# A four-layer graph stack on one core: the order of the small work among the first tiles, and neighbour counts on four quarters of the PE array

## The chip, the cores and the metric

The kernel runs on one core of one Trainium2 chip. The metric is device time in microseconds of the whole launch. A core has five engines with queues of their own: PE (matmul, with its weight loads shown apart as PEld), DVE (VectorE), ACT (ScalarE), POOL (GpSimd) and SP (SyncE, which here only issues DMAs).

## The reference

The graph has N = 3327 nodes with D = 64 features, `x` [N, D], and a dense matrix `adj` [N, N] of which well under 1% of the entries are not zero (all f32). Four layers follow each other, each `x = x + layer(relu(layernorm(x)))`:

```python
# layer 0: two gated cells, relu after each
m = adj @ (x @ W);  gi = m @ wih.T + bih;  gh = x @ whh.T + bhh
r = sigmoid(i_r + h_r); z = sigmoid(i_z + h_z); n = tanh(i_n + r * h_n)
x = (1 - z) * n + z * x
# layer 1: weights by the rank of a neighbour in its row
mask = (adj != 0);  rank = cumsum(mask, axis=1);  deg = rank[:, -1:]
k = minimum(deg, 100);  pos = rank - (deg - k)
w = mask * where(pos > 0, 0.5 ** (k - pos), 0);  out = w @ (x @ weight) + bias
# layer 2: three times  x = ((adj * adj) @ x) @ W.T + b
# layer 3: twice        x = tanh(concat([adj @ x, x]) @ W[k])
```

So `adj` is multiplied from the left eight times, k = 0 to 7 in the kernel. Layer 1 (k = 2) needs, for each row and each block of 128 columns, how many neighbours lie in later blocks: the counts that the change touches.

## The kernel before

The host pads `adj` to 3328 and passes it transposed. A node index is (s, b, p): half s of 2, block b of 13, position p of 128. Output nodes are cut into four chunks of blocks, `CH` = 0-3, 3-6, 6-9, 9-13, and into two groups of chunks, `GROUPS = [(0, 1), (2, 3)]`. A tile of `adj` is 128 sources q (26 of them) by the outputs of one group in both halves: 128 x 2 x 768 f32 for group 0 (768 KB), 128 x 2 x 896 for group 1 (896 KB). It lands in one of 20 slots. `propagate` (L607) multiplies a tile, chunk by chunk, into PSUM sums: the features of the 128 sources are the weights (128 x 64), the tile streams, and half s of the outputs goes to half s of the PE columns. Each f32 product is two passes in the trace, so a tile costs eight passes, four per chunk.

The loop: a list `units` of (k, chunk, tile) is written before anything is issued. `alone(0, 0, ...)` puts product k = 0 for group 0, `joint(1, 0, ...)` puts k = 0 for group 1 with k = 1 for group 1 a few tiles behind (`later`), so that a tile serves two products, and so on. The last `sweep` tiles go chunk by chunk. `run()` walks through `units`, issues loads up to 44 units ahead, masks (`make_mask`, L466: VectorE turns a tile into 0/1 bf16, in two halves), and then calls `propagate`. Small work stands in generators (`tasks`), advanced by `spend`, which charges PE time to each task: a `yield 1.5` waits for 1.5 us of products to be issued. Thus every engine's order of instructions is fixed when the program is written out; on the chip only semaphores decide when each starts. Loads are all on SP's queue in that order, with at most eight DMAs in flight (each waits for the one eight before it).

The counts: during k = 0, `count` (L542) multiplies each masked tile by `behind`, a 128-row matrix of ones and zeros whose window of D columns starts at NQ - 1 - q (NQ = 26). Row i of the result for half s sums over all tiles with q > i. For each of the two chunks of a group and each half there is one product with 64 weight columns (of which at most 26 carry counts) into PSUM rows `s * D`, and one bank per chunk. `Counting` holds `lag` tiles back and then issues one tile's counts after each tile. At the end `count_done` (L555) copies a bank to `totals`.

Before the first product: `before_0(c)` calls `layernorm_relu` (L834 to L849; the reciprocal root is on POOL, L845) for chunk c, then `transpose_to_features` (L791, ACT copies L793). The start-up loop `for c in (0, 0, 1, 0, 1, 2, 1, 2, 3, 2, 3, 3)` advances the four of them in turn. `more_constants` clears buffers on POOL, loads the cell weights (`load_cell`, L152 and L155, into `stage`), unfolds them (L162, copies L165, L167), folds two matrices (L175, L307), and computes one gate of the first cell ahead of time for each chunk (`ahead_of_cell`, L201). When k = 0 of a chunk ends, `after_0` runs its cell: `evacuate_stacked` (L824, L825), gates (L876), elementwise work (L881 to L908), back to nodes (L774, L944).

Of the kernel before, what the change touches and what calls it, by code (L numbers as in the profile page):

```python
# [44 lines left out]
N, D = 3327, 64  # L45
P = 128
NB = 13
NQ = 2 * NB
# [3 lines left out]
CH = [(0, 3), (3, 6), (6, 9), (9, 13), (3, 5), (5, 6)]  # L52
NC = 4
PARTS = (4, 5)
CWM = 512
GROUPS = [(0, 1), (2, 3)]
# [24 lines left out]
STREAM_US = 0.86  # L81
# [15 lines left out]
def kernel(  # L97
# [9 lines left out]
    nc = tc.nc  # L107
# [18 lines left out]
    stage = const.tile([P, 7 * D + NBIAS], F32, name="stage")  # L126
# [24 lines left out]
    def load_cell(cell):  # L151
        nc.sync.dma_start(out=stage[upper(0), :7 * D].rearrange("p (w f) -> p w f", f=D),  # L152
                          in_=weights[:, (W1, W2)[cell]:(W1, W2)[cell] + 7])
        if cell == 0:
            nc.sync.dma_start(out=stage[upper(0), 7 * D:], in_=bias_cols)  # L155
# [80 lines left out]
        yield from product(1, 2)  # L236

    def more_constants():
        nc.gpsimd.memset(stage, 0.0)
        nc.gpsimd.memset(cells, 0.0)  # L240
        for c in range(NC):
            for h in range(2):
                nc.gpsimd.memset(both[c][upper(h), h], 0.0)
        nc.gpsimd.memset(bd, 0.0)
        yield 5.0
        load_cell(0)
        yield 20.0
        unfold_cell(0)
        yield 1.0

        full = work.tile([P, P], BF16, name="t2")
        nc.gpsimd.memset(full, -TWO7)
        nc.gpsimd.affine_select(out=tri, in_=full, pattern=[[-1, P]], compare_op=ALU.is_gt, fill=0.0,
                                base=0, channel_multiplier=1)
        nc.gpsimd.affine_select(out=tri, in_=tri, pattern=[[-1, P]], compare_op=ALU.not_equal, fill=TWO7 * TWO7,
                                base=0, channel_multiplier=1)
        nc.gpsimd.memset(tri[:, P - 1:P], 0.0)
        nc.gpsimd.memset(bitsb, BITS)
        nc.gpsimd.memset(lasty, 0.0)
        wide = work.tile([P, P], F32, name="t2")  # L260
        nc.gpsimd.memset(wide, 0.0)

        for i, (bi, bh) in enumerate(((BI1, BH1), (BI2, BH2))):
            nc.vector.tensor_add(bsum[:, i], bcol[:, bi:bi + 2], bcol[:, bh:bh + 2])

        nc.vector.tensor_scalar(wide[0:D], wide[0:D], bcol[0:D, BL1:BL1 + 1], None, op0=ALU.add)
        yield 3.0
        i, ps = take()
        mm(ps[:, :D], wide, ident[:, :D])
        nc.vector.tensor_copy(brow[:, 3], ps[:, :D])  # L270
        give(i)
        yield 1.0
        yield from fold_cell(0)
        for c in range(NC):
            yield 1.0
            ahead_of_cell(c)
        yield 50.0
        load_cell(1)
        yield 20.0
        unfold_cell(1)  # L280
        yield from fold_cell(1)
        yield 30.0
        for h in range(2):
            nc.sync.dma_start(out=bd[upper(h), :, upper(h)], in_=weights[:, WL1:WL3])
            for i in range(2):
                nc.sync.dma_start(out=w3[upper(h), :, i], in_=weights[:, WL3 + (h + i) % 2:NW:2])
        yield 5.0
        nc.sync.dma_start(
            out=brow[:, 0:3],
            in_=bass.AP(tensor=bias_rows.tensor, offset=bias_rows.offset, ap=[[0, P], [D, 3], [1, D]]),  # L290
        )
        yield 22.0
        yield from fold_hops()
# [5 lines left out]
    def width(c):  # L299
        return blocks(c) * P  # L300
# [15 lines left out]
    def take(sums=False, either=True):  # L316


        either = either and not sums
        pool = idle_sums if sums else idle_temps  # L320
        if either and idle_sums and (not pool or released[idle_sums[0]] < released[pool[0]]):
            pool = idle_sums
        for c in list(tasks):
            if not pool and c not in running:
                advance(c)
        i = pool.popleft()
        return i, banks[i]
# [33 lines left out]
    def begin(c, task):  # L361
        finish(c)
        tasks[c] = [task, 0.0]
        advance(c)

    def finish(c):
        while c in tasks:
            advance(c)

    def later_task(us, task):  # L370
        yield us
        yield from task

    def spend(us):

        for c in list(tasks):
            if c in tasks and c not in running:
                tasks[c][1] -= us
                if tasks[c][1] <= 0:
                    advance(c)  # L380
# [79 lines left out]
    def make_mask(t, kind):  # L460

        t.mask = Mask(t.w)
        rows = P - 1 if kind == RANKED else P

        def piece(half):
            nc.vector.tensor_scalar(t.mask.view[:rows, half], t.view()[:rows, half], 0.0, None, op0=ALU.not_equal)  # L466
            if half == 0 and kind == RANKED:

                for ch in GROUPS[t.g]:
                    finish(("count", ch))  # L470
                nc.gpsimd.dma_start(out=t.mask.view[P - 1:P], in_=totals[t.g][t.q:t.q + D + 1:D, :])  # L471
            if half == 1:
                t.used()

        pieces.extend([(t, 0, piece), (t, 1, piece)])
# [54 lines left out]
    counts = {}  # L530
    squared = {}

    def count(t, first, last):


        mask_pieces(t=t)
        for c in GROUPS[t.g]:
            w = width(c)
            if first:
                counts[c] = take(either=False)  # L540
            for s in range(2):
                nc.tensor.matmul(counts[c][1][s * D:(s + 1) * D, :w], behind[:, NQ - 1 - t.q:NQ - 1 - t.q + D],  # L542
                                 t.mask.view[:, s, t.cols(c)], start=first, stop=last)
            spend(STREAM_US * w / CWM * 0.25)
            if last:
                begin(("count", c), count_done(c))
        t.mask.free()

    def count_done(c):
        g = c // 2  # L550
        w = width(c)
        w0 = (CH[c][0] - CH[GROUPS[g][0]][0]) * P
        i, ps = counts.pop(c)
        yield 0.8
        nc.scalar.copy(totals[g][:, w0:w0 + w], ps[:, :w])  # L555
        give(i)

    def last_sources(g):

        w = sum(width(c) for c in GROUPS[g])  # L560
        w0 = CH[GROUPS[g][0]][0] * P
        room = Mask(w)
        v = room.view.rearrange("p s w -> p (s w)").bitcast(F32)
        nc.gpsimd.memset(v, 0.0)  # L564
        yield 4.0
        rows = adjT.rearrange("(q p) (s n) -> q p s n", p=P, s=2)
        for s in range(2):
            nc.sync.dma_start(out=v[s * D:s * D + NQ], in_=rows[:, P - 1, s, w0:w0 + w])
        yield 12.0
        nc.vector.tensor_scalar(v, v, 0.0, 129.0 * TWO7, op0=ALU.not_equal, op1=ALU.mult)  # L570
        for c in GROUPS[g]:
            finish(("count", c))
        yield 1.0
        nc.vector.scalar_tensor_tensor(v, totals[g], -TWO7, v, op0=ALU.mult, op1=ALU.add)
        yield 1.5
        nc.scalar.activation(lastw[g], v, AF.Relu, bias=bitsb)
        room.free()
# [44 lines left out]
    class Counting:  # L622
# [3 lines left out]

        def add(self, t):
            self.waiting.append(t)
            if len(self.waiting) > self.lag:
                self.next()  # L630

        def next(self):
# [6 lines left out]
    def alone(g, k, sweep, lag=None, parts=False):  # L639
        tiles = [Tile(q, g, KIND[k] == SQUARED) for q in sources_of(*range(NC))]  # L640
        counting = Counting(g, lag)
        chunks = (GROUPS[g][0], *PARTS) if parts else GROUPS[g]
        for t in tiles[:NQ - sweep]:
            for c in chunks:
                put(k, c, t)
            if lag is not None:
                counting.add(t)
        for c in chunks:
            for t in tiles[NQ - sweep:]:
                put(k, c, t)  # L650
                if lag is not None and c == GROUPS[g][0]:
                    counting.add(t)
        counting.rest()
# [277 lines left out]
    def before_0(c):  # L931
        h = nodes(c)
        yield from layernorm_relu(h, c)
        y[0][c] = h
        yield 12.0 + 3.0 * c
        transpose_to_features(h, c)

    def after_0(c, acc):
# [84 lines left out]
    after[:] = [after_0, after_1, after_2, after_3, after_4, after_5, after_6, after_7]  # L1023


    alone(0, 0, sweep=2, lag=5)
    joint(1, 0, sweep=6, later=4, keep=3, lag=2)
    joint(0, 1, sweep=4, later=20, keep=0)
    joint(1, 2, sweep=6, later=6, keep=1)
# [3 lines left out]
    joint(1, 6, sweep=8, later=4, keep=4)  # L1033
    alone(0, 7, sweep=6, parts=True)

    for c in (0, 0, 1, 0, 1, 2, 1, 2, 3, 2, 3, 3):
        if c in tasks:
            advance(c)
        else:
            begin(c, before_0(c))  # L1040
    begin(NC, more_constants())
    begin(NC + 1, later_task(130.0, last_sources(0)))
    begin(NC + 2, later_task(155.0, last_sources(1)))
    run()
# [41 lines left out]
```

## Time and profile before

| | us |
|---|---|
| runs of the kernel | 706.61, 705.86, 706.64 (median 706.61) |
| profiled execution: span from first to last instruction (no other time of it is given) | 703.7 |
| PE busy | 679.8 |
| DVE, ACT, POOL busy | 350.1, 271.8, 80.0 |
| DMA: bytes moved, mean rate | 201.31 MB, 286 GB/s |

The span leaves out what lies ahead of the first and behind the last instruction: the median stands 2.9 us above it. A line of the profile's groups or of its chain names an engine, the destination tile and the line of the program; `L607` is thus the product of `propagate` whatever the tile. In the lines by stretches the columns are: stretch and length, busy us and (count) for PE, PEld, DVE, ACT and POOL, then the granted PE clock, the share of the DMA engines and GB/s. In the chain: start, length, what. In the list of waits: who waited for whom, us in total, times, longest. "Busy" of PE counts overlapping matmuls once, and their ends are modelled; two products on different halves of the columns run at the same time, so a mean duration of 0.49 us does not say that PE is held for so long.

### The profile page before, as it was taken

The page shows a single profiled execution, that of the slowest core. Times are in us where ns is not written, and L with a number is a line of the kernel's source. Part 1 is how long each engine was busy: PE and PEld are TensorE (multiplying, and loading weights), DVE is VectorE, ACT ScalarE, POOL GpSimd, SP SyncE. Part 2 cuts the span into 40 slices and gives each one's busy share as a digit, 9 for nine tenths or more (in the row PEclk, how much of TensorE's full clock was granted, in tenths as well). Part 3 has the DMA queues.
Part 4 walks back from the last instruction along what each step waited for, and adds up shares of the span by engine and source line. Part 5 has one row for each costly group of instructions (what it writes and reads, how often), then busy time and mean ns, then how long its engine had stood idle before and what let it go on. Part 6 is the DMA issues. An engine that isn't in the chain of part 4 may idle for free.

```text
span 703.7 us, 12628 instructions
## 1 busy us (share of the span) xinstructions
PE 679.8 (97%) x5100; PEld 372.9 (53%) x5100; DVE 350.1 (50%) x746; ACT 271.8 (39%) x422; POOL 80.0 (11%) x114
## 2 busy tenths in 40 slices
PE   1999999999999999999999999999999999999997
PEld 1454666643556787677444444333344444344586
DVE  7556835643997889847523105425271565005101
ACT  1014100122146888888998206832166600000101
POOL 4300000002284233111100000000000000000000
PEclk9999999999999999999999999999999999999999
DMA  9999996089686952683799649973998399927991
GB/s 344 401 385 404 406 405 241 2 314 398 209 279 253 371 177 76 246 297 96 265 390 343 245 151 409 405 276 100 398 366 271 107 391 406 406 81 276 402 403 45
DMA packets 68549, 201.31 MB, mean 286 GB/s; under 512 B 7228, under 2 KB 8228, under 8 KB 68492
## 3 DMA queue, kind: packets, MB, share of 16 engines
q1 hardware_dynamic: 65596, 199.46, 75.9%
q8 instruction: 40, 0.66, 0.4%
q10 hardware_dynamic: 720, 0.85, 0.3%
q0 software_dynamic: 2176, 0.20, 0.2%
q14 instruction: 17, 0.14, 0.1%
HBM read 199.45 MB, written 0.85 MB: 285 GB/s over the span
## 4 chain that ended last, share of the span: by engine, by line
PE 91%; DVE 7%; issue 0%; ACT 0%; DMA 0%; POOL 0%; ACTq 0%; DVEq 0%; POOLq 0%
PE sum L607 77%; PE temp L307 5%; PE temp L542 2%; PE temp L876 2%; PE sum L307 1%; DVE adj L466 1%; PE temp L774 1%; PE sum L876 1%; DVE e L521 1%; DVE st L842 1%; DVE adj L901 1%; DVE t L836 1%; DVE y L841 0%; DVE st L834 0%; DMA xs<-in_x 0%
## 5 line engine op out<-in xcount | busy, mean ns | idle before, releaser
L607 PE MATMUL sum<-adj,y 128*64 128x384 f32 (+3 forms) x3016 | 534.5, 502 | 0.7 <-DVE y L849 0.6
L607 PEld LDWEIGHTS sum<-adj,y 128*64 128x64 f32 x3016 | 243.5, 137 | 237.3 <-issue 212.4
L440 ACT ACTIVATE adj<-adj 128x768 f32<-128x768 f32 (+1 forms) x176 | 144.2, 893 | 45.8 <-PE sum L607 21.9
L466 DVE TENSOR_SCALAR adj<-adj 128x768 bf16<-128x768 f32 (+3 forms) x208 | 114.0, 597 | 39.8 <-PE temp L542 31.8
L824 ACT COPY both<-sum 64x384 f32<-64x384 f32 (+3 forms) x17 | 8.1, 478 | 192.6 <-PE sum L607 191.4
L607 PE MATMUL sum<-e,both 128*64 128x384 bf16 (+1 forms) x624 | 78.5, 339 | 0.5 <-DVE e L521 0.5
L523 ACT ACTIVATE e<-temp,bitsb 128x384 int16<-128x384 f32 (+1 forms) x117 | 66.0, 605 | 15.1 <-PE temp L307 9.9
L825 DVE COPY both<-sum 64x384 f32<-64x384 f32 (+3 forms) x17 | 9.6, 569 | 110.5 <-ACT both L824 110.5
L307 PE MATMUL temp<-adj,tri 128*64 128x384 bf16 (+1 forms) x332 | 56.8, 341 | 0.5 <-DVE e L521 0.2
L442 DVE TENSOR_TENSOR adj<-adj 128x768 f32<-128x768 f32 (+1 forms) x32 | 30.6, 1005 | 52.1 <-DMA adj<-in_adjT 33.4
L845 POOL TENSOR_TENSOR st<-st,mhalf 128x6 f32<-128x6 f32 (+1 forms) x16 | 24.0, 1498 | 283.2 <-DVE st L843 279.5
L607 PEld LDWEIGHTS <-both 128*64 128x64 bf16 x624 | 46.6, 110 | 15.5 <-issue 2.2
L307 PEld LDWEIGHTS <-tri 128*64 128x64 bf16 x416 | 33.5, 110 | 15.3 <-issue 7.1
L521 DVE TENSOR_SCALAR e<-temp 128x384 int16<-128x384 f32 (+1 forms) x49 | 30.1, 617 | 21.1 <-ACT e L523 10.5
L471 POOL DMA_DIRECT2D adj<-totals x52 | 31.5, 607 | 51.2 <-PE temp L307 40.9
L803 DVE STREAM_TRANSPOSE both<-y 32x96 f32<-32x96 f32 (+1 forms) x128 | 35.6, 278 | 2.9
L542 PE MATMUL temp<-adj,behind 128*64 128x384 bf16 x208 | 30.3, 339 | 0.9 <-DVE adj L466 0.7
L819 DVE STREAM_TRANSPOSE y<-t 32x96 f32<-32x96 f32 (+1 forms) x64 | 17.8, 278 | 24.9 <-ACT t L810 24.0
L542 PEld LDWEIGHTS <-behind 128*64 128x64 bf16 x208 | 17.0, 110 | 17.6 <-issue 15.9
L755 DVE COPY t<-sum 128x384 f32<-128x384 f32 x6 | 3.3, 555 | 35.3 <-PE sum L607 35.3
L564 POOL MEMSET adj<- 128x768 f32 (+1 forms) x2 | 1.9, 950 | 145.3 <-PE sum L607 145.3
L523 ACT ACTIVATE e<-sum,bitsb 128x384 int16<-128x384 f32 (+1 forms) x28 | 16.6, 598 | 2.5 <-PE sum L307 2.1
(132 smaller groups left out, 327.8 us busy)
## 6 DMA issues: line engine op xcount, KB each, us to landing
adj<-in_adjT SPq DMA_DIRECT2D x130, 768.0 KB, 8.5
adj<-in_adjT SPq DMA_DIRECT2D x104, 896.0 KB, 12.3
xs<-in_x SPq DMA_DIRECT2D x1, 640.0 KB
adj<-totals POOLq DMA_DIRECT2D x26, 3.0 KB, 5.1
adj<-totals POOLq DMA_DIRECT2D x26, 3.5 KB, 3.0
out<-xs ACTq DMA_DIRECT2D x2, 192.0 KB
out<-xs ACTq DMA_DIRECT2D x1, 256.0 KB
stage<-in_weights SPq DMA_DIRECT2D x2, 112.0 KB, 13.1
```

The source lines that it names most:

```text
L307: nc.tensor.matmul(out[hs], lhsT[:, hs], rhs, start=start, stop=stop)
L440: nc.scalar.activation(sq, v, AF.Square)
L442: nc.vector.tensor_tensor(sq, v, v, ALU.mult)
L466: nc.vector.tensor_scalar(t.mask.view[:rows, half], t.view()[:rows, half], 0.0, None, op0=ALU.not_equal)
L471: nc.gpsimd.dma_start(out=t.mask.view[P - 1:P], in_=totals[t.g][t.q:t.q + D + 1:D, :])
L521: nc.vector.tensor_scalar(wide[:, s], ps[:, :w], BITS, 0.0, op0=ALU.add, op1=ALU.max)
L523: nc.scalar.activation(wide[:, s], ps[:, :w], AF.Relu, bias=bitsb)
L542: nc.tensor.matmul(counts[c][1][s * D:(s + 1) * D, :w], behind[:, NQ - 1 - t.q:NQ - 1 - t.q + D], t.mask.view[:, s, t.cols(c)], start=firs ...
L607: nc.tensor.matmul(acc[h][1][h * D:(h + 1) * D, :w], yq[h], rhs[h], start=first and n == 0, stop=last and n == len(terms) - 1)
L803: nc.vector.transpose(to[at:at + 32, :, q], h[q * 32:(q + 1) * 32, :, s, f * 32:(f + 1) * 32])
L845: nc.gpsimd.tensor_tensor(st[:, 3, :n], st[:, 2, :n], mhalf[:, :n], ALU.pow)
L876: nc.tensor.matmul(ps[upper(1 - s), :w], cells[:, cell, s, g, :], both[c][:, s], start=True, stop=True)
```

## The change

Six edits, all in the code of the first 140 us.

1. The start-up loop advances chunk 0 first: `(0, 0, 0, 1, 0, 1, 1)`. Chunks 2 and 3 begin later, as tasks due after 4 and 10 us of products. In `before_0` the pause ahead of the transposition is 2.5 instead of 12 + 3c.
2. `stage` is cleared and `load_cell(0)` issued before `run()`, so ahead of all tile loads on SP's queue and behind the clearing on POOL's. The pauses of `more_constants` change with it.
3. A count product takes 32 weight columns instead of 64. The two chunks of a group and the two halves are four products with `tile_position=(0, 0)`, `(0, 32)`, `(0, 64)`, `(0, 96)`, into four quarters of the rows of one bank. Their number, 208, stays.
4. `Counting` issues the counts of two tiles together (`lag + 1`, two calls of `next`), and its `lag` for group 0 is 3 instead of 5.
5. `count_done` is one task per group: four copies, two on ACT and two on VectorE, into rows `s * D` to `s * D + 31` of `totals`. POOL clears `totals` beforehand, since only 32 of 64 rows are written.
6. `spend` is told half as much for counts.

```diff
--- before.py
+++ after.py
@@ -236,15 +236,14 @@
         yield from product(1, 2)
 
     def more_constants():
-        nc.gpsimd.memset(stage, 0.0)
         nc.gpsimd.memset(cells, 0.0)
         for c in range(NC):
             for h in range(2):
                 nc.gpsimd.memset(both[c][upper(h), h], 0.0)
         nc.gpsimd.memset(bd, 0.0)
-        yield 5.0
-        load_cell(0)
-        yield 20.0
+        for t in totals:
+            nc.gpsimd.memset(t, 0.0)
+        yield 4.5
         unfold_cell(0)
         yield 1.0
 
@@ -269,12 +268,12 @@
         mm(ps[:, :D], wide, ident[:, :D])
         nc.vector.tensor_copy(brow[:, 3], ps[:, :D])
         give(i)
-        yield 1.0
+        yield 1.5
         yield from fold_cell(0)
         for c in range(NC):
-            yield 1.0
+            yield 4.0
             ahead_of_cell(c)
-        yield 50.0
+        yield 47.0
         load_cell(1)
         yield 20.0
         unfold_cell(1)
@@ -466,8 +465,7 @@
             nc.vector.tensor_scalar(t.mask.view[:rows, half], t.view()[:rows, half], 0.0, None, op0=ALU.not_equal)
             if half == 0 and kind == RANKED:
 
-                for ch in GROUPS[t.g]:
-                    finish(("count", ch))
+                finish(("count", t.g))
                 nc.gpsimd.dma_start(out=t.mask.view[P - 1:P], in_=totals[t.g][t.q:t.q + D + 1:D, :])
             if half == 1:
                 t.used()
@@ -534,25 +532,31 @@
 
 
         mask_pieces(t=t)
-        for c in GROUPS[t.g]:
+        g = t.g
+        if first:
+            counts[g] = take(either=False)
+        for n, c in enumerate(GROUPS[g]):
             w = width(c)
-            if first:
-                counts[c] = take(either=False)
             for s in range(2):
-                nc.tensor.matmul(counts[c][1][s * D:(s + 1) * D, :w], behind[:, NQ - 1 - t.q:NQ - 1 - t.q + D],
-                                 t.mask.view[:, s, t.cols(c)], start=first, stop=last)
-            spend(STREAM_US * w / CWM * 0.25)
-            if last:
-                begin(("count", c), count_done(c))
+                at = (2 * n + s) * 32
+                nc.tensor.matmul(counts[g][1][at:at + 32, :w], behind[:, NQ - 1 - t.q:NQ - 1 - t.q + 32],
+                                 t.mask.view[:, s, t.cols(c)], start=first, stop=last, tile_position=(0, at))
+        spend(STREAM_US * t.w / CWM * 0.125)
+        if last:
+            begin(("count", g), count_done(g))
         t.mask.free()
 
-    def count_done(c):
-        g = c // 2
-        w = width(c)
-        w0 = (CH[c][0] - CH[GROUPS[g][0]][0]) * P
-        i, ps = counts.pop(c)
+    def count_done(g):
+        i, ps = counts.pop(g)
         yield 0.8
-        nc.scalar.copy(totals[g][:, w0:w0 + w], ps[:, :w])
+        for n, c in enumerate(GROUPS[g]):
+            w = width(c)
+            w0 = (CH[c][0] - CH[GROUPS[g][0]][0]) * P
+            for s in range(2):
+                at = (2 * n + s) * 32
+                (nc.vector.tensor_copy if s else nc.scalar.copy)(totals[g][s * D:s * D + 32, w0:w0 + w],
+                                                                 ps[at:at + 32, :w])
+            yield 0.8
         give(i)
 
     def last_sources(g):
@@ -568,8 +572,7 @@
             nc.sync.dma_start(out=v[s * D:s * D + NQ], in_=rows[:, P - 1, s, w0:w0 + w])
         yield 12.0
         nc.vector.tensor_scalar(v, v, 0.0, 129.0 * TWO7, op0=ALU.not_equal, op1=ALU.mult)
-        for c in GROUPS[g]:
-            finish(("count", c))
+        finish(("count", g))
         yield 1.0
         nc.vector.scalar_tensor_tensor(v, totals[g], -TWO7, v, op0=ALU.mult, op1=ALU.add)
         yield 1.5
@@ -626,7 +629,8 @@
 
         def add(self, t):
             self.waiting.append(t)
-            if len(self.waiting) > self.lag:
+            if len(self.waiting) > self.lag + 1:
+                self.next()
                 self.next()
 
         def next(self):
@@ -932,7 +936,7 @@
         h = nodes(c)
         yield from layernorm_relu(h, c)
         y[0][c] = h
-        yield 12.0 + 3.0 * c
+        yield 2.5
         transpose_to_features(h, c)
 
     def after_0(c, acc):
@@ -1023,7 +1027,7 @@
     after[:] = [after_0, after_1, after_2, after_3, after_4, after_5, after_6, after_7]
 
 
-    alone(0, 0, sweep=2, lag=5)
+    alone(0, 0, sweep=2, lag=3)
     joint(1, 0, sweep=6, later=4, keep=3, lag=2)
     joint(0, 1, sweep=4, later=20, keep=0)
     joint(1, 2, sweep=6, later=6, keep=1)
@@ -1033,12 +1037,16 @@
     joint(1, 6, sweep=8, later=4, keep=4)
     alone(0, 7, sweep=6, parts=True)
 
-    for c in (0, 0, 1, 0, 1, 2, 1, 2, 3, 2, 3, 3):
+    nc.gpsimd.memset(stage, 0.0)
+    load_cell(0)
+    for c in (0, 0, 0, 1, 0, 1, 1):
         if c in tasks:
             advance(c)
         else:
             begin(c, before_0(c))
     begin(NC, more_constants())
+    begin(2, later_task(4.0, before_0(2)))
+    begin(3, later_task(10.0, before_0(3)))
     begin(NC + 1, later_task(130.0, last_sources(0)))
     begin(NC + 2, later_task(155.0, last_sources(1)))
     run()
```

## The prediction

> **What bounds the kernel now.** First the page's busy line and the slices: TensorE is busy 97% of the span, the clock is granted, and the only empty stretches are at the two ends.
>
> ```profile
> PE 679.8 (97%) x5100; PEld 372.9 (53%) x5100; DVE 350.1 (50%) x746; ACT 271.8 (39%) x422; POOL 80.0 (11%) x114
> PE   1999999999999999999999999999999999999997
> DMA  9999996089686952683799649973998399927991
> ```
>
> So time is won by giving PE less work, or by starting it earlier, provided nothing else then ends last. The list of PE's waits gives the size of the second:
>
> ```profile
> PE temp L791 <- DVE y L849: 14.9, 1, 14.9
> ```
>
> PE's first instruction waits 14.9 us for VectorE, which runs all four chunks' norms before it finishes the first (`y L849` of chunk 0). The chain of waits in order of time shows what follows: the first 48 passes take 9.19 us, later ones 1.29 per eight, and the tail of the first phase hangs on DVE, not PE.
>
> ```profile
> 14.41 0.47 DVE y L849
> 14.92 1.55 PE temp L791 x12
> 16.47 9.19 PE sum L607 x48
> 25.99 1.29 PE sum L607 x8
> ...
> 66.33 0.48 ACT both L824
> 66.83 0.57 DVE both L825
> ...
> 79.61 0.69 PE sum L774 x22
> 80.58 1.50 PE sum L607 x8
> 82.08 0.38 PE temp L542 x4
> ```
>
> Third, the stretches: here the DMA column matters.
>
> ```profile
> 0.00:15.00 15.00, 0.08 (x2) 0.08 (x4) 11.09 (x26) 1.28 (x1) 5.68 (x14) 1.00 0.88 333
> 15.00:66.20 51.20, 51.20 (x394) 26.36 (x396) 29.76 (x63) 9.08 (x17) 9.35 (x19) 1.00 1.03 396
> 66.20:80.30 14.10, 13.21 (x122) 8.30 (x118) 13.00 (x26) 4.72 (x9) 0.00 (x0) 1.00 1.03 406
> 80.30:131.20 50.90, 50.90 (x322) 35.44 (x318) 24.99 (x47) 0.47 (x1) 0.00 (x0) 1.00 0.74 285
> ```
>
> In the first 80 us both PE and the DMA engines are full. PE started late, so tiles lay ready for it. A tile of group 0 is 0.786 MB, at 0.400 MB/us 1.95 us of DMA, while PE spends 1.29 (eight passes) + 0.32 (its counts) = 1.61. **A PE that starts early catches up with the DMA.**
>
> **What the Trainium skill says.** (1) "TensorEngine Tiling (Array Packing)", Tiling Modes: 128x32 gives four independent tiles, and changing the tiling mode, not just the tile, drains TensorE. Every matmul of the kernel before has the form `128*64`, so its trace shows neither four quarters nor a mode switch. (2) "TensorE: Matmul & The Clock Gate", Part 3: matmuls on different column tiles overlap, three tiles of 32 columns gaining 2.38 times. The trace agrees for two halves: four counts of 326 ns each advance PE by 0.32, so one of a pair costs 0.16 of streaming and 0.166 is a tail that the next one overlaps. (3) Same page, the clock gate: about 3.4 us of activity pass at half rate before the full clock. The trace agrees: 48 passes took 9.19, where 6 x 1.29 = 7.74, 1.45 lost; this start-up cost moves, it doesn't go.
>
> **The change part by part.**
>
> *One norm first.* VectorE's order in the changed program is norm of chunk 0, half of chunk 1's, then chunk 0's closing L849. By the rows of before: statistics end at 5.95, GpSimd's power runs 6.04 to 7.38, L849 takes 0.5: y of chunk 0 at 7.9. PE's first work is now the products of tile 1, not the transposition.
>
> *Weights at the head of the queue.* SP, after the two loads of x, now waits for GpSimd's memset of `stage` (ends about 2.5: after L148 at 1.79 + 0.19, and 0.48 long), then issues weights and biases (0.61 the shorter L152, 0.60 L155) and reaches tile 1 at 3.7 instead of 1.75. Bytes flow 1.7 after an issue (0.98 MB by 5.0 at 0.396 puts the start at 2.5; first issue 0.81). x and weights fill the engines until 4.9, tile 1 flows from 5.4: 0.5 lost. The weights' bytes are not extra, only earlier. Tile 1 (0.852 MB of x + 0.118 + 0.786) lands at about 7.5, so PE starts near 8, against 14.9. Behind SP's wait stands every tile load.
>
> *What the early start is worth.* Until tile 26: 0.852 + 0.118 + 26 x 0.786 = 21.4 MB. Before: 5.0 MB by 15.0, the rest at 0.396, so tile 26 lands at 56.4; after, 56.9. Three chunk products follow it in the sweep, 3 x 0.65 + 0.17 = 2.1: end of the phase at **59.0 by DMA**. By PE: 7.9 + 1.45 cold + 26 x 1.29 + 26 x 0.16 of counts + 6.5 of small work (L791 2.85, L162 0.35, L201 2.81, folding 0.5, from the chain) = 53.6, plus about 1.4 where the first counts wait for masks (VectorE's L165 waits for a PE product behind tile 4, and masks 1 to 2 stand around it) = 55.0, plus 13 visits to the new mode. With 0.33 a visit (below): **59.3**. Before: 66.2. Gain 6.9.
>
> Then the gates. From the last copy L825 to y of layer 1 before: 66.8 to about 80.8, DVE busy 13.0 of 14.1. Its instructions after: eight mask halves instead of ten, two new copies of `totals` instead: I take 0.4 more. PE covers this with five tiles, gates and counts (about 13.4), whose last tile lands at 56.9 + 5 x 2.27 = 68.3, ahead of need at 73.5. So **6.5** of the 6.9 reaches 80.6.
>
> *Counts on quarters.* Per tile in group 0, 2 x 0.16 becomes 0.16; in group 1 0.38 becomes 0.21. Fully overlapped: 26 x 0.16 = 4.2 us in each group. In group 0 the DMA hides it. In group 1 (80 to 140) DMA is ahead (tile 26 of it lands at 56.9 + 59 = 116, PE needs it at about 123), so it counts. Against it, mode switches. Counts come two tiles at a time, so 13 visits per group, two switches each. Bounds of a visit: nothing; or on both switches the 0.166 tail and the weight load (0.11 or 0.14) exposed, 0.6. Below nothing is excluded: a switch can't make streaming quicker. I take two tails, **0.33**, with the loads hidden: group 1 then gives 4.2 - 13 x 0.33 = -0.1, nothing. PE's issue rate doesn't limit: 24 passes of L774 take 0.7, 29 ns each, and quarters need one per 40.
>
> *Small rest.* Two bank-wide ACT copies per group become two on ACT and two on DVE of 32 rows (about 0.5 each): DVE's pair of group 1 falls where it is busy 25 of 50.9. `totals` memsets stand on GpSimd ahead of chunk 2's power, about 0.5 each; that power waits for VectorE's statistics anyway. Earlier norms of chunks 2 and 3 fit among masks (1.03 a tile against DMA's 1.95). Without that slack each microsecond of them would delay a count and then PE. The pacing's lower price of counts shifts some DVE and ACT instructions up to the ranked stage; the order of PE after that is the same by kind of instruction. I put all this at 0, with +-1.
>
> *Sum.* 6.5 + 0.1 - 0: span 703.7 - 6.5 = 697.2. The profiled execution has no other time than its span; the median of the runs, 706.6, stands 2.9 above, which I keep: **700.0**. After 131 us PE is busy 564.4 of 568.8, so what is won stays won.
>
> **Rivals.**
> - *The switch is free*, hardware hides it as it hides other weight loads. For: bf16 and f32 products alternate in the trace with no gap. Against: the skill's sentence. First phase ends at 59.0 (DMA), counts give 4.2: 6.8 + 4.2 = 11, **695.6**.
> - *Drain and load both show*, 0.6 a visit: first phase 55.0 + 7.8 = 62.8, gain 3.4 - 0.4; group 1 loses 13 x 0.6 - 4.2 = 3.6. Net nothing: **about 707**; half-way (0.45), 61 and 1.7 lost, **703.5**.
> - *Slower: the new mode costs more than a serial switch*, or quarters overlap only in twos (0.32 more per visit), on PE at L542 between products. It decides from 0.6 a visit; at 0.9: first phase 66.7, group 1 -7.5, gates -0.4: 8.4 lost, **715**. Against: the two halves overlap fully today.
> - *The change doesn't do what it says*: PE, waiting for tiles, drops to the cold clock again. Each cold tile costs 2.6, more than the DMA's 1.95; ten such cost 6.5 and leave **706**. Against: PE would still be over 85% busy.
>
> **How the numbers follow.** Forecast (698 to 702.5) 0.45; free switch (695 to 698) 0.25; half-exposed or partly cold start (702.5 to 707) 0.18; slower 0.12. A measurement of this kernel can tell about 0.2% (1.4 us) from no change. Below 705.2: 0.45 + 0.25 + 0.13 = 0.83; within: 0.06; above 708.0: 0.11. The range leaves out the slower case and little at the fast end: 695 to 706.5.
>
> **What would show it.** Right: PE's first idle near 8; L607 then waiting for `DMA adj<-in_adjT` among tiles 5 to 26; the copy L829 at about 59 to 60; layer 1's first product near 74; forms `128*32` for L542, with 0.2 to 0.4 of PE idle or stretched at each visit. Wrong: L829 after 63 (visits dearer or a cold clock: look at the spacing of L607's passes); no gap around L542 (a free switch, 696); or an early start given back after 130 us, as PE idle that before didn't have.

## The result, and the profile after

The change made the kernel slower: 709.13 us (708.96 to 709.37) against 706.24 for the kernel before in the same runs, a ratio of 1.0037 (95% interval 1.0025 to 1.0049). Forecast were 700.0 in a range of 695.0 to 706.5. The profiled execution spans 707.5 us, 3.8 more than before; 0.9 of this lies in the one execution that was profiled before (703.7, where 86 others of that kernel span 703.0 to 706.2 with a median of 704.6).

The page's busy line and slices, as shown of before:

```profile
PE 681.3 (96%) x5100; PEld 348.3 (49%) x5100; DVE 351.3 (50%) x750; ACT 272.4 (39%) x422; POOL 75.6 (11%) x116
PE   4998799999999999999999999999999999999997
DMA  8999995179686952593899739972998399917991
```

PE starts earlier (first slice 4, it was 1), but there are two new dips in the first 90 us, one of them at the fifth slice. PE's waits name them (who waited for whom, us in total, times, longest):

```profile
PE sum L610 <- DMA adj<-in_adjT: 9.6, 2, 9.0
PE temp L542 <- DVE adj L465: 5.5, 4, 2.9
```

The start now waits for the first tile (9.0), no longer for VectorE (14.9). The new wait is PE at the counts, for masks: 5.5 us where it had 0.7. In stretches (length, then busy us and count of PE, PEld, DVE, ACT, POOL, PE clock, DMA share, GB/s):

```profile
9.00:61.40 52.40, 50.90 (x386) 22.43 (x388) 33.49 (x77) 7.55 (x15) 13.81 (x22) 1.00 1.03 402
61.40:82.90 21.50, 16.08 (x110) 6.88 (x109) 14.19 (x28) 6.15 (x12) 0.00 (x0) 0.92 1.03 407
82.90:131.20 48.30, 48.30 (x330) 16.90 (x328) 24.76 (x45) 0.08 (x1) 0.00 (x0) 1.00 0.73 279
```

The gates' stage of the first cell took 14.1 us before. Here 21.5 pass from the end of chunk 1's products to the copy of layer 1's first nodes (L948, 82.9), and PE idles for 5.4 of them. The granted clock is 0.92 in this stage, where it was 1.00. PE's timeline of it (start, length, what; in brackets the idle time ahead and its releaser):

```profile
63.31 0.66 PE L542 MATMUL temp<-adj,behind 128*32 128x384 bf16 x9
64.93 1.28 PE L542 MATMUL temp<-adj,behind 128*32 128x384 bf16 x7 [0.96 <-DVE adj L465]
66.14 0.87 PE L610 MATMUL sum<-adj,y 128*64 128x384 f32 x4
66.84 2.10 PE L880 MATMUL temp<-both,cells 128*64 128x384 f32 x12
...
75.70 0.86 PE L542 MATMUL temp<-adj,behind 128*32 128x384 bf16 x4 [1.12 <-DVE adj L465]
79.49 0.62 PE L542 MATMUL temp<-adj,behind 128*32 128x384 bf16 x3 [2.93 <-DVE adj L465]
80.04 1.55 PE L610 MATMUL sum<-adj,y 128*64 128x384 f32 x4
81.37 0.85 PE L778 MATMUL sum<-ident,both 128*64 128x64 f32 x12
```

Chunk 1's gates (L880 at 66.84) come behind a pair of counts that waits for the last masks, and behind half of group 1's first tile. Later PE stands at group 1's first pair of counts, of which the second tile's mask comes late; chunk 0's way back to nodes (L778), which needs nothing of that mask, is behind it in the queue. ACT and VectorE in the same stage:

```profile
67.70 1.23 ACT L885 ACTIVATE adj<-temp,bsum 128x384 f32<-128x384 f32 x2 [4.00 <-PE temp L880]
68.83 0.45 ACT L557 CAST totals<-temp 32x384 bf16<-32x384 f32 x1
...
69.31 0.55 DVE L557 CAST totals<-temp 32x384 bf16<-32x384 f32 x1 [2.31 <-ACT totals L557]
```

VectorE, which had been busy for 13.0 of the stage's 14.1 us before, stood 2.3 us at its first new copy of `totals`. That copy was written behind ACT's, ACT's is behind chunk 1's gates in ACT's queue, and those waited 4.0 us for PE.

One more view is used throughout: the start of PE's n-th matmul in the trace (n counted from 0), less that of the kernel before. Every kernel here issues 5100, so it shows where a lead was won or lost. (Around n = 500 and 900 the order of counts and products differs between kernels; n = 400, 800 and the end compare well. One execution is compared with one other, so the last column need not be the difference of the medians.)

| n (time before, us) | 1 (15) | 200 (42) | 400 (67) | 800 (127) | 1000 (153) | last (699) |
|---|---|---|---|---|---|---|
| changed kernel | -5.9 | -5.5 | -3.2 | +2.0 | +2.3 | +3.5 |

The early start is real, half of it is left at 67 us, and 5.2 us are lost in the gates' stage. (The stage is longer by 7.4 us from event to event. The table compares equal numbers of matmuls instead: at the stage's start PE had issued 388 of them, 396 before, and 498 against 518 at its end.)

### The profile page after: what moved, and what is told of

It reads as the page before. It is cut to its first block, busy times and chain, and to the rows that moved or that the text cites. A ratio compares the mean times of both kernels' runs of the same rounds, so it can differ in the third digit from the quotient of the medians.

```text
span 707.5 us, 12615 instructions
## 1 busy us (share of the span) xinstructions
PE 681.3 (96%) x5100; PEld 348.3 (49%) x5100; DVE 351.3 (50%) x750; ACT 272.4 (39%) x422; POOL 75.6 (11%) x116
## 4 chain that ended last, share of the span: by engine, by line
PE 64%; DVE 3%; ACT 1%; issue 1%; POOL 0%; ACTq 0%; DVEq 0%; POOLq 0%
PE sum L610 57%; PE temp L306 5%; PE sum L306 1%; PE temp L778 1%; DVE e L519 1%; ACT e L521 1%; DVE adj L465 1%; PE temp L880 1%; PE sum L880 0%; DVE both L829 0%; ACT both L923 0%; DVE st L846 0%; POOL st L849 0%; DVE xs L1023 0%; ACT t L1020 0%
## 5 line engine op out<-in xcount | busy, mean ns | idle before, releaser
L610 PEld LDWEIGHTS sum<-adj,y 128*64 128x64 f32 x3016 | 228.0, 138 | 272.3 <-issue 241.5
L306 PE MATMUL temp<-adj,tri 128*64 128x384 bf16 (+1 forms) x334 | 53.8, 341 | 1.6 <-ACT e L521 0.9
L542 PE MATMUL temp<-adj,behind 128*32 128x384 bf16 x208 | 17.4, 348 | 6.3 <-DVE adj L465 5.5
L880 PE MATMUL temp<-both,cells 128*64 128x384 f32 (+1 forms) x80 | 18.5, 520 | 0.3 <-DVE both L829 0.3
L542 PEld LDWEIGHTS <-behind 128*32 128x32 bf16 x208 | 4.4, 94 | 24.6 <-issue 23.6
```

Source lines behind the costliest of these rows:

```text
L306: nc.tensor.matmul(out[hs], lhsT[:, hs], rhs, start=start, stop=stop)
L542: nc.tensor.matmul(counts[g][1][at:at + 32, :w], behind[:, NQ - 1 - t.q:NQ - 1 - t.q + 32], t.mask.view[:, s, t.cols(c)], start=first, sto ...
L610: nc.tensor.matmul(acc[h][1][h * D:(h + 1) * D, :w], yq[h], rhs[h], start=first and n == 0, stop=last and n == len(terms) - 1)
L880: nc.tensor.matmul(ps[upper(1 - s), :w], cells[:, cell, s, g, :], both[c][:, s], start=True, stop=True)
```

## The experiments

All times are medians. Each ratio is against the kernel before, run on the same chip beside it (706.4 to 706.8), with its 95% interval. Two experiments compared with each other often ran on different chips; their difference then carries both intervals, about 1 us together. "Lead" is the last table's difference with its sign turned.

**Halving the change: the start alone, the counts alone.**

```diff
 e1: the change without edits 3 to 6 (counts, lag, copies and price as before)
 e2: the change without edits 1 and 2 (start and pauses as before)
```

> The start-up edits alone (chunk 0's norm first, weights at the head of the queue, the new pauses); the counts stay as before, on halves, one tile at a time, one copy per bank on ACT. My theory: the early start is real, limited by the landing of the tiles (about 61 to 62 us for the end of group 0's first product, 66.2 before), and it is lost afterwards to the new count code in the gates' stage. Without that code the gates take the 14 to 15 us that they took before, layer 1's first product starts 4 to 5 us earlier than before, and the run gives 702 us (701 to 703.5). Rival: the early start can't be kept, because masks of tiles that have not landed stand ahead of the gates' elementwise work on VectorE; then VectorE waits for DMA between 62 and 80 us and the run gives 706 us or more.

Measured: 710.69 us, ratio 1.0053 (1.0038 to 1.0068). Slower, and yet not by the rival's mechanism: the lead was 2.6 us at n = 400 and 2.5 at 800, so the gates' stage lost nothing; 5.2 us went between n = 1200 and 1400, and 1.7 more by 1600. The list of PE's waits has one long entry there:

```profile
PE sum L604 <- DVE brow L232: 4.4, 1, 4.4
```

The folding of the last layers' weights came 21.5 us sooner than before (its first product, L224, at 201.4 instead of 222.9), because the pauses of edit 2 are written for edit 6's half price of counts, which e1 lacks. L232, a copy of that folding, stood behind seven mask halves on VectorE (4.81 us from 204.14), and PE behind L232. From 208.2 to 215.0 the granted clock was half, which is an estimated 2.9 us of PE's time after the wait (half of 209.1 to 215.0). e1 is thus confounded by pacing.

> The count edits alone (quarters, two tiles at a time, four copies, cleared totals, half price in the pacing); the start as before. Theory: a visit of two tiles costs PE about the same as four pairs did before (0.5 to 0.7 us against 0.64 to 0.75), so the products give nothing, and the gates' stage loses as in the changed kernel: the copy of totals on VectorE waits for the one on ACT and the pair of counts waits for masks behind the gates; 2 to 5 us lost, 709 to 711 us. Rival: the loss in the gates' stage came from the tiles' late landing, not from the count code; then 706 us, with the gates taking 14 us.

Measured: 713.19 us, ratio 1.0090 (1.0066 to 1.0115). The theory's place was right, its size too small: 7.1 us lost between n = 400 (lead 1.5) and 800 (5.6 behind), PE waiting 6.0 us at L545 (the counts) for masks. The tiles' late landing is not the cause: between 55 and 90 us neither PE nor VectorE waited for a load here. e2 is confounded too, the pauses of before under half price put the folding late (L224 is matmul 1626 of the trace, 1481 before).

**The copies of totals.**

```diff
-(nc.vector.tensor_copy if s else nc.scalar.copy)(totals[g][s * D:s * D + 32, w0:w0 + w], ...)
+nc.scalar.copy(totals[g][s * D:s * D + 32, w0:w0 + w], ...)
```

> The changed kernel, but all four copies of totals on ACT. Theory: in the changed kernel VectorE stood 2.3 us at its copy of totals, which waited for ACT's copy, itself behind the gates of chunk 1; without it the gates' stage is 2 to 3 us shorter and the run gives 706 to 707 us. Rival: VectorE's wait is only moved (its next instruction needs chunk 1's gates anyway) and the paired counts still wait for masks: no change, 709 us.

Measured: 705.61 us, ratio 0.9983 (0.9972 to 0.9994); against the changed kernel 3.5 us less, more than the theory's 2 to 3. VectorE's next instruction now waits for ACT's gates itself:

```profile
68.37 0.62 DVE L890 SCALAR_TENSOR_TENSOR adj<-adj,bcol,adj 128x384 f32<-128x384 f32 x1 [1.32 <-ACT adj L885]
```

In the changed kernel this L890 started at 69.90, with PE's gates at the same time to within 0.05 us. So the rival is right for part of the 2.3 us: 1.3 of waiting stay, and the copy itself cost 1.5. At n = 800 e3 stands 1.8 us better than the changed kernel; another 1.1 comes by n = 1000, where group 1's copies fall into the gates of chunks 2 and 3. PE still waits 4.4 us for masks.

**The change of tiling.**

```diff
 on e2 (counts only):
-            if len(self.waiting) > self.lag + 1:
-                self.next()
-                self.next()
+            if len(self.waiting) > self.lag:
+                self.next()
-    alone(0, 0, sweep=2, lag=3)
+    alone(0, 0, sweep=2, lag=5)
```

> The start as before; counts on quarters, but one tile at a time with the lags of before, so that PE changes its tiling 104 times instead of 52. Theory: a change in and out costs 0.2 to 0.3 us per visit beyond the products' own streaming, so 26 more visits cost 5 to 8 us against the counts-only kernel, less what the pairs' wait for masks cost there (3 us): 711 to 715 us. Rival: changes of the tiling are free, and the run is faster than the counts-only kernel, 703 to 706 us.

Measured: 718.81 us, ratio 1.0185 (1.0158 to 1.0211), more than forecast by the theory. The total isn't the price of the tiling: the second cell's folding came forward (its first L162 is matmul 528 of the trace, 1008 in e2; `take` advances waiting tasks when no PSUM bank is idle, but that a shortage of banks did it is not shown), PE idled 3.3 us from 85 to 100, and the clock was half from 71.8 to 78.6. The steady part of group 1 gives the price. A visit is a stretch of counts between two stretches of products. PE's timeline of the kernel before, of e5 and of the changed kernel, two visits each:

```profile
98.73 0.65 PE L542 MATMUL temp<-adj,behind 128*64 128x384 bf16 x4
99.11 3.27 PE L607 MATMUL sum<-adj,y 128*64 128x384 f32 x16
102.12 0.65 PE L542 MATMUL temp<-adj,behind 128*64 128x384 bf16 x4
```

```profile
104.95 0.40 PE L545 MATMUL temp<-adj,behind 128*32 128x384 bf16 x4
105.28 3.23 PE L613 MATMUL sum<-adj,y 128*64 128x384 f32 x16
108.44 0.40 PE L545 MATMUL temp<-adj,behind 128*32 128x384 bf16 x4
```

```profile
87.36 0.61 PE L542 MATMUL temp<-adj,behind 128*32 128x384 bf16 x8
87.91 6.23 PE L610 MATMUL sum<-adj,y 128*64 128x384 f32 x32
94.07 0.62 PE L542 MATMUL temp<-adj,behind 128*32 128x384 bf16 x8
```

The kernel before needs 3.39 us a tile, of which the products take 3.01 (99.11 to 102.12) and the counts 0.38. A period is 3.49 for one tile in e5 and 6.71 for two in the changed kernel. Less the products, one tile's counts with a visit take 0.48 and two tiles' counts with a visit 0.69. So a tile's counts on quarters stream for 0.21, the time of one stream of 512 columns (0.16 x 512 / 384): the four quarters overlap fully. A visit costs 0.27. Before, the counts took 0.38, the sum of their two streams (0.16 + 0.21): a visit without a change of form costs nothing that shows. Paired quarters win 0.03 us a tile, single ones lose 0.10.

**Pairing alone.**

```diff
 on the kernel before:
-            if len(self.waiting) > self.lag:
+            if len(self.waiting) > self.lag + 1:
+                self.next()
                 self.next()
-    alone(0, 0, sweep=2, lag=5)
+    alone(0, 0, sweep=2, lag=3)
```

> The kernel before, with the counts of two tiles issued together (and a lag of 3 for group 0), but still as products of 64 columns on halves, with the copies of before: no change of tiling. Theory: the pairing by itself makes PE wait for masks that stand behind the gates on VectorE; 3 to 5 us lost at the first product of layer 1, 709 to 711 us. Rival: the loss of the counts-only kernel (6 us) was the change of tiling and the copies: 706.6 us here.

Measured: 707.91 us, ratio 1.0020 (1.0012 to 1.0028). The theory missed its size: pairing costs some 1.4 us by itself, PE's wait for masks is 2.0 us instead of e2's 6.0. So the long wait needs more than the pairing. It doesn't need the copies on VectorE, for e3 has none there and waits 4.4; among the other differences, the pacing and the quarters, no run decides.

**The place of the first pair.**

```diff
 on e3 (copies on ACT):
+            self.seen += 1
-            if len(self.waiting) > self.lag + 1:
+            if len(self.waiting) > self.lag + 1 and (self.g == 0 or self.seen > 4):
```

> As the kernel with all copies of totals on ACT, and the first pair of counts of group 1 comes one tile later, behind tile 5 of the group and behind chunk 0's way back to nodes (L778), where it stood ahead of both. Theory: PE's in-order queue stood 4.4 us at that pair, whose second mask is behind the gates on VectorE, while tile 5 and L778 were ready; after the wait the clock was half for 4 us. With the pair later the wait falls below 1.5 us, the clock stays full, and the run gains 2 to 4 us on the kernel with copies on ACT: 702 to 704 us. Rival: VectorE's chain of the gates sets the end anyway, and the wait only moves to the first product of layer 1: no change, 705.6 us.

Measured: 703.83 us, ratio 0.9962 (0.9951 to 0.9974), 1.8 us below e3, at the short end of the theory. PE's wait for masks fell from 4.4 to 1.8. The wait went partly elsewhere (1.1 for layer 1's nodes), and in its profiled execution the clock still fell to 0.73 between 80 and 85 us. (The expectation's 4 us at half clock are 3.4 in the trace.) How much of the 1.8 is the clock is asked below.

**The first weights on another queue.**

```diff
 on e3:
+        queue = nc.sync if cell else nc.scalar
-        nc.sync.dma_start(out=stage..., in_=weights...)
+        queue.dma_start(out=stage..., in_=weights...)
```

(and the same for the biases)

> As the kernel with all copies of totals on ACT, but the first cell's weights and biases are issued on ACT's queue, so that no tile load waits behind the clearing of stage. Theory: tile 1 is issued at 1.75 instead of 3.7 us, lands about 1 us earlier, and group 0's last tile as well; 0.5 to 1.2 us gained against the kernel with copies on ACT, 704.5 to 705. Rival: the DMA engines' bytes set the landing of tile 26, and the order of issue changes nothing: 705.6 us.

Measured: 704.44 us, ratio 0.9972 (0.9963 to 0.9981), 1.2 us below e3: the theory's upper end, but the two intervals overlap, so by this run alone a price of the weights at the head of the tiles' own queue is not shown.

**Both repairs, then the gates sooner.**

```diff
 e10: e7 and e8 together
 e11, on e10, in gru:
-        yield 0.8 * pace
+        yield (0.3 if cell == 0 and c == 1 else 0.8) * pace
```

> The two repairs together: copies of totals on ACT, first pair of group 1 one tile later, and the first weights on ACT's queue. Theory: they act at different places (the gates' stage and the landing of the tiles), so they add: 1.8 and 1.2 us off the kernel with copies on ACT (705.6), 702.6 us (701.5 to 703.5). Rival: both shorten the same wait of the gates' stage; then no better than the better one alone, 703.8 us.

Measured: 702.14 us, ratio 0.9941 (0.9926 to 0.9955), below either repair alone, as the theory has it.

> As the kernel with both repairs, and the pause between chunk 1's evacuation and its gates in the first cell is 0.3 instead of 0.8 us of products, so that its gates stand ahead of the last pair of counts and of group 1's first tile. Theory: with counts priced at half, these gates had slipped behind a pair of counts that waits for the last masks (0.96 us) and behind a half tile; ACT then waited 4.0 us for them, 2.5 us more than in the kernel with the start-up edits alone. With the gates sooner layer 1 starts 1.5 to 2.5 us earlier: 700.5 to 701.5 us. Rival: VectorE's own sequence of masks and elementwise work sets the end of the stage, and ACT's wait was free: no change, 702.6 us.

Measured: 700.91 us, ratio 0.9920 (0.9905 to 0.9934), better than both kernels. First two lines of e10's timelines (PE, ACT), then e11's:

```profile
66.42 2.10 PE L884 MATMUL temp<-both,cells 128*64 128x384 f32 x12
67.29 1.23 ACT L889 ACTIVATE adj<-temp,bsum 128x384 f32<-128x384 f32 x2 [4.00 <-PE temp L884]
```

```profile
62.37 0.51 PE L544 MATMUL temp<-adj,behind 128*32 128x384 bf16 x8
62.82 1.78 PE L884 MATMUL temp<-both,cells 128*64 128x384 f32 x7
...
73.50 0.87 PE L782 MATMUL temp<-ident,both 128*64 128x64 f32 x24
...
75.29 0.40 PE L544 MATMUL temp<-adj,behind 128*32 128x384 bf16 x3 [0.21 <-DVE adj L467]
```

```profile
64.31 1.23 ACT L889 ACTIVATE adj<-temp,bsum 128x384 f32<-128x384 f32 x2 [1.55 <-PE temp L884]
```

Chunk 1's gates start at 62.8 instead of 66.4, ACT's wait for them is 1.55 instead of 4.00, the way back to nodes stands at 73.5 instead of 75.2. The lead at n = 800 is 4.7 us, 2.3 in e10. VectorE's own sequence was not the bound. With four runs on each side the 1.2 us between the medians is a rough figure.

The length of the gates' stage in the traces, from the end of chunk 1's products to the first copy of layer 1's nodes, shows the repairs one by one:

| | before | changed | e3 | e7 | e8 | e10 | e11 |
|---|---|---|---|---|---|---|---|
| us | 14.1 | 21.5 | 18.9 | 17.6 | 18.1 | 17.6 | 15.8 |

Of these stages two ran in part at half clock: 3.4 us of the changed kernel's, 1.9 of e3's.

**The clock in these runs.** In the traces of the changed kernel, e2, e3 and e7 the granted clock was half once for 3.4 us (from 79.3, 83.4, 78.4 and 79.3). In a run of 705 us this takes 0.0024 off the mean, so a run with a mean of 0.999 or 1.000 had no such fall. The kernel before, whose clock falls in its trace only behind the last product (at 701.9), is at 0.998 to 1.000 in all of 86 runs, so a run at 0.997 or less had a fall further ahead. Three of the four runs of the changed kernel are there. Medians by the mean clock, with the number of runs (those at 0.998 can be either and are left out):

| | e3 | e7 | e8 | e10 |
|---|---|---|---|---|
| 0.997 or less | 705.6 (12) | 705.4 (2) | 705.1 (11) | none |
| 0.999 or more | 703.3 (1) | 703.6 (5) | 703.1 (6) | 702.1 (3) |

The fall goes with 1.8 to 2.0 us (e7, e8). At equal clock e7 and e8 are within 0.5 us of e3: most of what each seemed to win over e3 is that fewer of their runs had the fall. Both together (e10) win about 1 us at full clock as well, by three runs against e3's one.

**What the start is worth beside the old counts.** Three kernels with edits 1 and 2 and the counts of before, now with the pause matched to full price:

```diff
 e6:  on e1   -        yield 47.0   +        yield 58.0
 e12: on e6, first weights and biases on ACT's queue, as in e8
 e13: on e6   -        yield 58.0   +        yield 60.0
```

> As the start-up edits alone, but the pause ahead of the second cell's weights is 58 instead of 47 us of products, so that the folding of the last layers' weights stands where it stood before (PE's order has it within 41 rows of the place before). Theory: with the start-up edits alone the first product of layer 1 was 2.5 us early, and the loss came at 200 us, where PE waited 4.4 us behind a folding pulled forward ahead of its weights' landing; without that the 2.5 us stay: 704 us (703 to 705). Rival: the early start brings its own loss later whatever the folding does (loads and slots out of step): 708 us or more.

Measured: 706.59 us, ratio 1.0001 (0.9992 to 1.0010). Between the theory and its rival. The lead of 2.7 us held to n = 800 and was 1.0 at 1000. There PE waited for the nodes of chunk 2:

```profile
PE sum L604 <- DVE y L941: 1.6, 1, 1.6
```

On VectorE the second cell's small copies (L165, L184, L185) stood ahead of that L941 and waited for PE's folding; in the kernel before they stand behind it. (The expectation's reason for e1's wait, weights not landed, was not right either: it was the seven mask halves.)

> The start-up edits with the folding in its old place and with the first weights on ACT's queue; the counts as before, on halves, one at a time. It tells what the quarters are worth beside the same start. Theory: 1 us better than without the ACT queue (706.6): 705.6 us, and 3 to 5 us behind the best kernel with paired quarters, of which the products' own saving is only 0.9 us in group 1 (26 tiles, 3.39 against 3.355 us). Rival: the start is worth the same with either kind of counts once its waits are gone; then 702 us.

Measured: 706.64 us, ratio 1.0004 (0.9995 to 1.0012). No better than e6, though at n = 400 to 800 its lead was 0.5 larger; the same wait of 1.6 us came, and more was lost later.

> The start-up edits alone with a pause of 60 instead of 58 ahead of the second cell's weights: with 60 the second cell's small products and the folding of the last layers stand at the same rows of PE's order as in the kernel before (573 and 806), and their copies on VectorE stand behind chunk 2's return to nodes again. Theory: with 58, 1.7 us of the 2.7 won by the start were lost at 144 us, where PE waited 1.6 us for chunk 2's nodes behind those copies; with 60 they stay: 704 us (703 to 705). Rival: what an early start wins in this kernel is lost again beyond 150 us whatever the order: 706.5 us.

Measured: 704.15 us, ratio 0.9967 (0.9953 to 0.9981). With the small tasks back at their rows the lead of 2.8 holds at n = 1000 to 1400; 1.0 goes by 1600. The start is worth 2.2 us.

**The second cell later, on e11.**

> The kernel with both repairs and the gates sooner, with a pause of 49 instead of 47: the second cell's copies stand behind chunk 2's return to nodes on VectorE. Theory: the lead over the kernel before falls from 4.7 to 5.4 and back at this place by about 1 us; a gain of 0 to 1.5 us, 699.5 to 701. Rival: PE has cover there and the later folding costs more at 190 us: 701 to 702 us.

```diff
 on e11:
-        yield 47.0
+        yield 49.0
```

Measured: 700.89 us, ratio 0.9924 (0.9908 to 0.9940): no gain over e11.

## Why the prediction was wrong, point by point

The span was forecast at 697.2 and came out at 707.5, 10.3 us apart. (The step from span to median was taken as 2.9; in every execution with both figures it is 1.7 to 2.3. And in the sum group 1's 0.1 is a loss, written as a gain. Neither decides anything.)

- **What bounds the kernel; the start.** Right in kind. Y of chunk 0 was ready as worked out, and no cold spell came among the tiles. The size was off. Tile 1 landed at 9.0, not 7.5. Tile 26 released PE at 59.2; its bytes were through at 56.8, as forecast, but a tile counts when its DMA has landed, 2.4 us after the stream's arithmetic says. This late landing cost PE only 0.6: after tile 1 it waited for no other load, so it caught up with the DMA at the last tile and not from tile 5 on. Chunk 1's products ended at 61.4 instead of 59.3: gain 4.8 instead of 6.9.
- **The new order at the head of SP's queue.** Costed at 0.5 us for the landing of the tiles, and in the traces tile 26 landed at 59.15 instead of 58.67. What taking it away brings in the total is not settled: 1.2 us (e8 against e3, not clear of noise), 1.7 (e10 against e7), nothing beside the old counts (e12 against e6).
- **The gates' stage.** This is the step that failed. "I take 0.4 more" counted VectorE's instructions and let PE cover the stage; it did not follow which queue each new instruction stands in and what that queue waits for. The stage took 7.4 us more than before. Moving the copies off VectorE shortens it by 2.6 (e3) and the run by 3.5, the second group's copies included. Putting chunk 1's gates ahead of the last pair shortens it by 1.8 (e11 against e10) and the run by some 1.2. The first pair behind L778 shortens it by 1.3 against e3, whose clock fell inside the stage, and by 0.5 where both clocks were full (e8 and e10); in the run it is not separable from the clock, whose fall, 1.8 to 2.0 us, came in this stage or just behind it. e11's stage is still 1.7 longer than that of before, without a cause named. That chunk 1's gates slipped is the "lower price of counts" which I had put at 0: it moved no work, but it let a later product slip ahead of the gates.
- **"Small rest" at 0, with +-1.** Copies and pacing were put here, as covered. The cover named for group 1's copies was VectorE's mean (busy 25 of 50.9), not the stage in which they fall. The changed kernel loses some 1.5 us more after n = 800.
- **Counts on quarters.** Right. By the sums above quarters overlap fully, a visit costs 0.27 us against 0.33 taken, and group 1's products win 26 x 0.03 = 0.8 us, an estimate from the steady part, where nothing was forecast. The kernels with both the start and repaired quarters lead the start alone (e11 against e13) by 3.2 us, more than this 0.8; 1.4 of it is there at n = 400. What the rest is, no run singles out.
- **"What is won stays won."** Only if the paced small work keeps its place. e6 and e13 differ by a pause of 2, and by 2.4 us.
- **The rivals.** Slower came true, but not through the rival named for it (a dear change of tiling). The cold clock of the last rival came too, but in the gates' stage and not among the tiles. None of the rivals was a queue blocked by a small instruction; the loss that came was missing from the list.

The Trainium skill's "TensorEngine Tiling (Array Packing)", Tiling Modes, has a change of mode drain TensorE. The trace agrees that a switch costs: some 0.13 us each, half of a visit's 0.27. The skill's page "TensorE: Matmul & The Clock Gate", Part 1, puts the return to half rate after an idle window of about 3.4 us. These traces show falls after shorter waits. In the changed kernel PE idled 2.9 us ahead of 79.5 and 1.1 shortly before, and the granted clock averaged 0.93 and 0.73:

```profile
75.00:80.00 5.00, 1.23 (x7) 0.30 (x6) 4.81 (x10) 0.52 (x1) 0.00 (x0) 0.93 1.02 405
80.00:85.00 5.00, 5.00 (x64) 3.11 (x64) 1.62 (x3) 0.00 (x0) 0.00 (x0) 0.73 1.03 406
```

That is 0.07 x 5 + 0.27 x 5 = 1.7 us of clock in this execution, near the 1.8 to 2.0 that the runs show. e8 had nearly the same wait (2.8 the longest) at full clock, and e7 and e10 had the same waits (1.1 the longest), e7 with the fall and e10 without, so it is no fixed price.

Left open: when such waits bring the fall of the clock and when not, why e11's stage is still 1.7 us longer, and the 1.0 us that e13 loses at about 230 us.

## What to carry to other kernels

When a stage has one engine without slack, follow each new instruction through its own queue: what stands ahead of it there, and what that waits for. A copy split over two engines "to share the load" can tie the busy one to the other's queue, and a batch of two needs its second input before its first is let go. Where small work is paced by a price of the main work, a changed price is a changed order: before a part of such a change is measured alone, put the small work back into its old place, or the comparison measures the pacing. And set runs of equal granted clock side by side: two repairs that seemed to win 1 to 2 us had mostly kept the clock up more often.

## What the runs showed of the hardware that was not expected

- Going from 64-column to 32-column products and back cost PE 0.27 us a visit, by one tile's counts (0.48) and two tiles' (0.69) together; four quarters streamed a tile's counts in 0.21 us, two halves in 0.38.
- With up to eight loads in flight tile 26's landing (59.2) came 2.4 us after as many bytes had been moved as it and all loads ahead of it have (56.8).
- The PE clock fell to half for 3.4 us after a longest wait of 2.8 to 2.9 us (changed kernel, e2, e3), and in one execution of 1.1 us (e7); for 6.8 us in e1 (4.4) and e5 (1.5). In the profiled execution of e8 it did not fall after a wait of 2.8, in that of e10 not after 1.1.
- Such a fall goes with 1.8 to 2.0 us of a run's time (e7, e8, runs grouped by their mean clock).
